# A two-layer kernel: layer 0's last FFN halves spread between layer 1's first projections, and the last batch's end in another order

## The chip, the cores and the metric

The kernel runs on one core of a Trainium2 chip. The metric is the device time of one execution in microseconds (us). A core has five engines with an instruction queue each: TensorE (PE, matrix products; its weight loads are listed apart as PEld), VectorE (DVE), ScalarE (ACT), GpSimd (POOL) and SyncE (SP), which issues most of the DMAs here. Engines run side by side and wait for each other through semaphores; each takes its own instructions strictly in order. On-chip data lie in SBUF, results of matmuls in PSUM banks of 128 x 512 fp32.

## What is computed

Four batches of 512 tokens with 512 features pass through two layers. Each layer is `x = x + s * silu(f)`, where s is a token mixer and f an FFN, both on the layer-normed x:

```python
xn = _layernorm(x)
s = _L0_attn_ref(xn, ...)          # 32 heads of 16, 8 key/value heads, softmax
g = _silu(_L0_ffn_ref(xn, ...))    # Hadamard-folded gated FFN, inner size 2048
x = x + s * g
xn = _layernorm(x)
s = _L1_attn_ref(xn, ...)          # gated delta rule, 6 heads of 64, short convolutions
g = _silu(_L1_ffn_ref(xn, ...))    # sign weights, relu, inner size 2048
x = x + s * g
```

The delta rule's recurrence over tokens, `S = S * exp(g_t) + k_t u_t`, with `u_t = b_t * (v_t - k_t S)`, is computed in four tiles of 128 tokens per batch: inside a tile by triangular inverses, between tiles through the state S.

## The kernel before

Names: NB = 4 batches, TB = 4 token tiles of 128 in a batch, NI = 16 slices of 128 of the inner size, VC = 3 slices of 128 of the 384 value columns. A Tile scheduler places the instructions: it keeps each queue's instructions close to the order in which the program lists them, and moves one past another where it takes that to be better, unless it is wrapped in `tc.keep_in_program_order`. Tiles come from pools; a tile of a pool waits until the buffer that it reuses is free, and a new pool waits until the pools whose space it takes are closed and their last readers are done.

**Layer 0.** Attention works in NU = 256 units u (64 per batch): `maxima(u)` (scores and row maxima), LAG = 11 units later `exps(u - 11)` (scores again as st, L433, and the exponentials on ACT, L435), and after every eighth `values` (L443; its sums go through DRAM and come back as the tiles oTc). The FFN is cut into as many pieces, `ffn(v, 0)` and `ffn(v, 1)` with v = u - LATE, LATE = 16: two halves in each unit, so that PE has work while DVE and ACT do the softmax. In a batch's second 32 pieces a half is one fp32 matmul of the down projection (`y<-wdn,hT`, L344; the profile lists two records for it, or four for a pair). After u = 255 there are no maxima left, and the loop goes on with the last exponentials and two halves each until `u == NU + LAG + 2`. What then is left of batch 3, four halves, four times `layer_sum` (x1 = x + s * g: four matmuls L475, a multiply on DVE L477, an add on POOL L479, a store) and four times `norm1` (statistics L61 and L62 on DVE, normalise L73, four transposes L489, a copy on ACT, a store to xn1_d, from which layer 1 loads batch 3 later), stands in `end_of_layer0()`.

**Between the layers.** `att.close()` frees the space of the attention; there the pools ce (SBUF) and cps (three PSUM banks, tiles named pu) are opened. Layer 1's first load, xn1T of batch 0 (L597), goes into ce, and so do wba and the first weights wp (L611). `projections(0)` is listed as steps with weights; then `end_of_layer0()` runs, then the steps, then `l0.close()`. Only then are c0, d0, dps and dpy opened, in which layer 1's FFN lives. There the constants upsc, drow, osc and woT are loaded on ACT's queue, and `drow * osc` (L877) is one instruction of DVE.

`projections(b)` is: `gate1(b, 2)` (L759, with the columns for the decays), `decays`, then for n = 0 to 8 `project(b, n)` (four matmuls L710, the profile shows eight records; a copy on ACT L716, three convolution steps on DVE L718, Tanh on ACT L722, a multiply on DVE L723 that ends the tile yc or yv) and `to_tokens(b, n - 1)` (four transposes L734 of yc, square and copy on ACT, a reduction on DVE), and last `gate1(b, 0)` and `gate1(b, 1)`.

**Layer 1's FFN** is a list of 128 pieces `up1(b, c)` and `down1(b, c)`, issued between the other steps: `part(count)` closes a stretch of steps in which count pieces are spread by the steps' weights. From the stretch `TAIL[1]` on, the pieces' order is pinned. `up1` begins for each batch by splitting xn1T into xsh and xsl (L892, L894). `down1(b, 15)` ends a batch: for each token tile t a multiply of y with drow (L964) into a tile named hT, of which there are two buffers, Tanh on ACT (L966), a multiply (L967) and a store to g1_d.

**The last batch's tail.** In `recurrence(3)` tile t needs `blocks32`, `blocks32b`, `blocks64` (the inverse's blocks), `with_state` (L1144, L1150: products with the state S), `new_values` (L1159, copied on ACT to Xv, L1162), `state` (S for the next tile), `outputs` (L1183), `out_norms`, `gated` (og), `project_out` (loads x1 and g1, three transposes L1222 of og, copied on ACT to ogT, L1224) and `project_out2` (six records L1233, then L1234 and L1236 on DVE and the store to out). The tiles 0 to 2 are projected out one to two steps behind the recurrence, tile 3 after it:

```python
recurrence(b)
for t in range(TB - 1, TB):
    add(0.4, project_out, NB - 1, t)
    add(2.6, project_out2, NB - 1, t)
part(len(pieces), True)
```

Of the kernel before, what the change touches and what calls it, by code (L numbers as in the profile page):

```python
# [33 lines left out]
def kernel(ctx: ExitStack, tc: tile.TileContext, i: dict, out: bass.AP):  # L34
# [66 lines left out]
    if True:  # L101
# [263 lines left out]

        sets = [(b, g) for b in range(NB) for g in range(HG)]
        NU, LAG, LATE = 8 * len(sets), 11, 16
        qds, qTs, nmxs, qms, pes = {}, {}, {}, {}, {}
# [125 lines left out]
        piece, zp = [0], []  # L494
        first_set()
# [25 lines left out]
        for u in range(NU + LATE):  # L521
            b, r = u // 64, u % 64
            v = u - LATE
            piece[0] = max(v, 0)
# [11 lines left out]
            if v >= 0:  # L536
                ffn(v, 0)
                ffn(v, 1)
# [21 lines left out]
            if u == NU + LAG + 2:  # L560
                break

        def end_of_layer0():
            for v in range(NU + LAG + 3 - LATE, NU):
                piece[0] = v
                ffn(v, 0)
                ffn(v, 1)
            for t in range(TB):
                layer_sum(NB - 1, t)
            for t in range(TB):  # L570
                norm1(NB - 1, t)
# [232 lines left out]
    def projections(b, between=(), done=None):  # L804
# [19 lines left out]
        for n in range(9):  # L824
            if done is not None and n % 2 == 0 and n < 2 * TB:
                add(0.0, gated, done, n // 2)
            prefetch()
            add(3.4, project, b, n)
            some()
            if n == 1:  # L830
                add(0.3, decay_sums, b)
            if n:
                add(0.45, to_tokens, b, n - 1)
                some()
            if done is not None and n % 2 and n < 2 * TB:
                add(0.4, project_out, done, n // 2)
                some(1)
                add(2.6, project_out2, done, n // 2)
        for m in range(VC - 1):
            prefetch()  # L840
            add(3.6, gate1, b, m)
            some()
            if m == 0:
                add(0.45, to_tokens, b, 8)
                some()
                add(0.0, norms, b)
# [4 lines left out]
    end_of_layer0()  # L851
    for _, f, args in steps:
        f(*args)
    steps.clear()
# [66 lines left out]
    pin = [False]  # L921
# [27 lines left out]

    def down1(b, c):  # L950
# [10 lines left out]
        if c == NI - 1:  # L961
            for t in range(TB):
                v = new(d0, [P, DM], F32, "hT")
                nc.vector.tensor_tensor(v, yss[b][t], drow, ALU.mult)  # L964
                th = new(d0, [P, DM], F32, "sw", bufs=3)
                nc.scalar.activation(th, v, AF.Tanh, scale=0.5)  # L966
                nc.vector.scalar_tensor_tensor(v, th, 1.0, v, ALU.add, ALU.mult)  # L967
                nc.sync.dma_start(g1_d[ds((b * TB + t) * P, P), :], v)
# [185 lines left out]
    def new_values(b, t):  # L1154
# [7 lines left out]
        nc.scalar.copy(X, px[:, :VD])  # L1162
# [30 lines left out]
    def out_norms(b, t=None):  # L1193
# [6 lines left out]
        nc.scalar.activation(so, so, AF.Sqrt)  # L1200
# [11 lines left out]

    def project_out(b, t):
        s = st[b]
        tok = ds((b * TB + t) * P, P)
        x1 = new(c0, [P, DM], F32, "x1l", bufs=2)
        nc.sync.dma_start(x1, x1_d[tok, :])
        g1 = new(c0, [P, DM], F32, "g1l", bufs=2)
        nc.sync.dma_start(g1, g1_d[tok, :])
# [5 lines left out]
        s["x1", t], s["g1", t] = x1, g1  # L1225

    def project_out2(b, t):
        s = st[b]
        tok = ds((b * TB + t) * P, P)
        x1, g1, ogT = s["x1", t], s["g1", t], s["ogT", t]  # L1230
        pf = bank()
        for m in range(VC):
            nc.tensor.matmul(pf, ogT[:, m, :], woT[:, m, :], start=(m == 0), stop=(m == VC - 1))  # L1233
        nc.vector.scalar_tensor_tensor(g1, pf, 0.5, g1, ALU.mult, ALU.mult)  # L1234
        eng = nc.vector if b >= NB - 2 else nc.gpsimd
        eng.tensor_tensor(x1, x1, g1, ALU.add)  # L1236
        nc.sync.dma_start(out[tok, :], x1)
# [18 lines left out]
    def recurrence(b, ahead=None, between=(), behind=0):  # L1256
# [9 lines left out]
        for t in range(TB + 2 if ahead is not None else TB + 1):  # L1266
# [24 lines left out]
            if 0 < t <= TB:  # L1291
                add(1.0, state, b, t - 1)
                add(1.0, outputs, b, t - 1)
                if t == TB - 1 and ahead is None:
                    add(2.0, with_state, b, t)
                    add(1.0, blocks64, b, None, t)
                if t - 1 + NZ < TB:
                    add(0.0, load_UT, b, t - 1 + NZ)
                if ahead is None:
                    if t == 3:  # L1300
                        part(TAIL[2], True)
                    add(0.0, out_norms, b, t - 1)
                    add(0.0, gated, b, t - 1)
                    for n in range(t - 3, t - 2 if t < TB else TB - 1):
                        if n >= 0:
                            add(0.4, project_out, b, n)
                            add(2.6, project_out2, b, n)
# [24 lines left out]
    for t in range(TB):  # L1332
# [6 lines left out]
        add(2.6, project_out2, b - 1, t)  # L1339
    while between:  # L1340
# [7 lines left out]
    for t in range(TB - 1, TB):  # L1348
        add(0.4, project_out, NB - 1, t)
        add(2.6, project_out2, NB - 1, t)  # L1350
# [59 lines left out]
```

## Time and profile before

| | us |
|---|---|
| median of 3 runs | 1506.74 |
| the runs | 1503.43, 1506.74, 1508.0 |
| the profiled execution | 1506.05 |
| its span | 1504.3 |
| mean granted clock of PE, as a share of full speed | 0.988 |

| stretch of the profile (us from the span's start) | PE busy, us | length, us |
|---|---|---|
| 1000 to 1100, layer 1 | 97.13 | 100 |
| 800 to 840, first projections | 28.60 | 40 |
| 840 to 880 | 38.76 | 40 |
| 1420 to 1440 | 17.18 | 20 |
| 1480 to 1504, the end | 15.95 | 24 |

How to read it: the first table compares the profiled execution with the undisturbed runs; the difference between its time and its span, 1.75 us, lies around the span. The second table gives for a stretch how long PE worked on matmuls. A stretch that PE fills can only become shorter by less work; a stretch with idle time, by letting PE wait for less. A granted clock below 1.00 makes the same matmuls longer while PE still counts as busy.

### The profile page before, as it was taken

How to read it: one execution, taken by the hardware profiler on the slowest of the kernel's cores; microseconds unless marked ns; L12 is line 12 of the kernel's file. 1: busy time of each engine (PE TensorE's matmuls, PEld its weight loads, DVE VectorE, ACT ScalarE, POOL GpSimd, SP SyncE). 2: the span in 40 equal slices, each digit the busy share in tenths (PEclk: the TensorE clock that was granted, in tenths of full speed). 3: DMA queues.
4: the chain of work that ended last, by engine and by line, in shares of the span. 5: the costliest groups of instructions: out<-in, count | busy, mean ns of one | idle time of the engine just before them, and what ended most of it. 6: DMA issues, size and time to landing. Idle time of an engine off the chain costs nothing. (4 is left out here: it accounts for less than half of the span.)

```text
span 1504.3 us, 22710 instructions
## 1 busy us (share of the span) xinstructions
PE 1434.3 (95%) x8144; PEld 856.0 (57%) x8144; DVE 1031.5 (69%) x1865; ACT 714.8 (48%) x1051; POOL 308.2 (20%) x301
## 2 busy tenths in 40 slices
PE   7999999999999999999998899999999999999997
PEld 3565533555335543456334566787568765776684
DVE  7999655765556655666516659668965799477646
ACT  4655554666446654566443424424352345323433
POOL 1122100322003210133101130054112521151000
PEclk9999999999999999999999999999999999999989
DMA  8865300474116630166014443435463354425423
GB/s 306 317 224 215 124 25 21 169 238 160 28 35 196 228 129 25 63 224 218 19 33 144 127 124 108 114 84 157 123 172 85 99 156 130 126 56 173 137 76 109
DMA packets 201793, 199.11 MB, mean 132 GB/s; under 512 B 65520, under 2 KB 153040, under 8 KB 200784
## 3 DMA queue, kind: packets, MB, share of 16 engines
q1 hardware_dynamic: 198624, 196.29, 41.4%
q10 hardware_dynamic: 3056, 1.37, 0.3%
q8 instruction: 64, 1.05, 0.3%
q14 instruction: 49, 0.40, 0.1%
HBM read 146.80 MB, written 46.19 MB: 128 GB/s over the span
## 5 line engine op out<-in xcount | busy, mean ns | idle before, releaser
L413 DVE TENSOR_REDUCE nmx<-sc 128x2 f32<-128x1024 f32 x256 | 312.1, 1219 | 160.9 <-PE st L433 149.7
L435 ACT ACTIVATE pe<-st 128x1024 f16<-128x1024 f32 x256 | 262.6, 1026 | 143.5 <-PE st L433 141.7
L344 PE MATMUL y<-wdn,hT 128*128 128x512 f32 x512 | 252.5, 617 | 3.0 <-DVE g L348 1.7
L326 PE MATMUL mm<-xr,wc 128*128 128x512 f32 x768 | 206.4, 410 | 0.0
L326 PEld LDWEIGHTS mm<-xr,wc 128*128 128x128 f32 x768 | 137.3, 189 | 48.6 <-issue 22.4
L337 POOL TENSOR_TENSOR hT<-hT,th 128x512 f32<-128x512 f32 x64 | 83.9, 1311 | 318.9 <-ACT hT L336 300.1
L344 PEld LDWEIGHTS y<-wdn,hT 128*128 128x128 f32 x512 | 87.1, 189 | 97.1 <-issue 89.7
L710 PE MATMUL pu<-xn1T,wp 128*128 128x512 f32 x288 | 133.1, 606 | 0.0
L934 PE MATMUL ph<-xsh,sg 128*128 128x512 f32 x256 | 113.6, 444 | 5.5 <-ACT sg L919 5.2
L412 PE MATMUL sc<-kT,qT 32*128 32x512 f16 x512 | 102.3, 384 | 6.3 <-DVE nmx L413 5.7
L934 PE MATMUL ph<-xsl,sg 128*128 128x512 f32 x256 | 105.5, 412 | 0.7 <-DVE xsl L894 0.7
L919 ACT ACTIVATE sg<-sw 128x512 fp32r<-128x512 f32 x128 | 79.4, 625 | 52.4 <-PE y L955 25.2
L433 PE MATMUL st<-qm,kT 32*128 32x512 f16 x512 | 100.3, 385 | 0.3 <-ACT pe L435 0.3
L459 POOL TENSOR_TENSOR oT<-os,sm 128x512 f16<-128x512 f32 x32 | 41.5, 1298 | 286.7 <-DMA sm<-rec_d 235.3
L412 PEld LDWEIGHTS <-qT 32*128 32x128 f16 x512 | 26.1, 91 | 130.0 <-issue 125.6
L710 PEld LDWEIGHTS pu<-xn1T,wp 128*128 128x128 f32 x288 | 54.9, 195 | 57.7 <-issue 55.9
L939 ACT ACTIVATE hT<-ph,upsc 128x512 f32<-128x512 f32 x64 | 43.8, 684 | 88.0 <-PE ph L934 88.0
L955 PE MATMUL y<-sg,hsh 128*128 128x512 f32 x256 | 83.9, 436 | 1.2 <-ACT sg L919 1.2
L326 PE MATMUL mm<-xr,fo 128*128 128x512 f32 x256 | 74.6, 426 | 0.5 <-DVE fo L257 0.5
L997 POOL TENSOR_TENSOR gm<-g,le 128x384 fp32r<-128x384 f32 x64 | 56.5, 901 | 88.7 <-PE pu L998 57.6
L955 PE MATMUL y<-sg,hsl 128*128 128x512 f32 x256 | 73.5, 398 | 0.0
L332 ACT ACTIVATE th<-mm,hwg 128x512 f32<-128x512 f32 x64 | 44.0, 688 | 58.3 <-PE mm L326 57.3
(291 smaller groups left out, 2364.0 us busy)
## 6 DMA issues: line engine op xcount, KB each, us to landing
wc<-wS SPq DMA_DIRECT2D x96, 512.0 KB
wS<-fo SPq DMA_DIRECT2D x16, 1024.0 KB
sw<-in_upT SPq DMA_DIRECT2D x64, 256.0 KB
sw<-in_downT SPq DMA_DIRECT2D x64, 256.0 KB
sm<-rec_d SPq DMA_DIRECT2D x128, 64.0 KB
raw<-in_w_gateT SPq DMA_DIRECT2D x8, 512.0 KB
hT<-in_w_downT SPq DMA_DIRECT2D x16, 256.0 KB
raw<-in_w_upT SPq DMA_DIRECT2D x8, 512.0 KB
```

The source lines that it names most:

```text
L326: nc.tensor.matmul(pgs[m], wcs[b, c, m][:, h, k, :], xrs[b][:, k, :], start=(k + h == 0), stop=(k == KC - 1 and h == 1))
L337: nc.gpsimd.tensor_tensor(hT, hT, ths[b, c], ALU.mult)
L344: nc.tensor.matmul(ys[t], hTs[b, c][:, ts(t, P)], wdn[:, c, :], start=(c == 0), stop=(c == NI - 1))
L412: nc.tensor.matmul(sc[:, j, :], qTs[n][rows, ts(t, P)], kTs[b, g // 4][rows, :], start=True, stop=True)
L413: nc.vector.tensor_reduce(nmxs[n][:, t, 2 * pr : 2 * pr + 2], sc, AX.X, ALU.max, negate=True)
L433: nc.tensor.matmul(st[:, j, :], kTs[b, g // 4][rows, ts(k, P)], qms[n][rows, :], start=True, stop=True)
L435: nc.scalar.activation(pes[u], st, AF.Exp)
L710: nc.tensor.matmul(pp, wps[b, n][:, k, 0:P], xn1Ts[b][:, k, :], start=(k == 0), stop=(k == KC - 1))
L919: tc.keep_in_program_order(nc.scalar.activation(sgs[b, c, m], raws[b, c, m], AF.Sign))
L934: ins = nc.tensor.matmul(ph, sgs[b, c, 0][:, ts(k, P)], xss[b][n][:, k, :], start=(k + n == 0), stop=(k == KC - 1 and n == 1))
L955: ins = nc.tensor.matmul(yss[b][t], hss[b, c][n][:, ts(t, P)], sgs[b, c, 1], start=(c + n == 0), stop=(c == NI - 1 and n == 1))
L997: nc.gpsimd.tensor_tensor(gm, bc_in(s["g2"][:, t, u, x], P), bc_mid(le, 3), ALU.mult)
```

## The change

**Layer 0's end.** `halves(u)` gives the number of halves issued before unit u. Up to u = NU it is two per unit as before; from there one per unit, and the loop ends at NU + LAG. The list `rest` holds the twenty halves left over, then the four `layer_sum` and the four `norm1`; they are called between the steps of `projections(0)`, in proportion to 1.5 times the steps' weights, so that `rest` is used up after two thirds of them. `end_of_layer0` is gone; `l0.close()` still comes after the steps.

**The last batch's end.** `project_out` is split: `out_loads` takes the loads of x1 and g1, `out_sum` the last multiply, the add and the store. For the last batch:

- `down1(3, 15)` only multiplies y with drow, pinned, into four buffers (two of hT, two of hsh). The rest of the piece, `gate_y2` (Tanh, multiply, store of g1), and `out_loads` come for all four tiles in a later step. The loads for tiles 2 and 3 go into the freed tile of xn1T.
- `project_out` of tiles 0 and 1 comes ahead of the last `with_state`; `project_out2` of tiles 0 to 2 comes after the last `outputs`, and `out_sum` behind it, pinned; its result banks are those of y (dpy) instead of pu.
- Tile 3's X is copied on DVE instead of ACT; Sqrt in `out_norms` of tiles 2 and 3 is pinned.
- The adds of `out_sum` run on POOL for tiles 0 to 2 and on DVE for tile 3.
- The weight of `blocks64` in the last stretch is 4 instead of 1, the stretch `TAIL[2]` ends at t = 3 behind the last `blocks64`, and `out_norms` and `gated` of tile 2 are listed after it.

```diff
+        def halves(u):
+            return 2 * (min(max(u, LATE), NU) - LATE) + max(u - NU, 0)
...
+        def half(h):
+            piece[0] = h // 2
+            ffn(h // 2, h % 2)
...
-        for u in range(NU + LATE):
+        for u in range(NU + LAG + 1):
...
-            if v >= 0:
-                ffn(v, 0)
-                ffn(v, 1)
+            for h in range(halves(u), halves(u + 1)):
+                half(h)
...
-            if u == NU + LAG + 2:
-                break
-        def end_of_layer0():
...
+        rest = [(half, h) for h in range(halves(NU + LAG + 1), 2 * NU)]
+        rest += [(f, NB - 1, t) for f in (layer_sum, norm1) for t in range(TB)]
...
     projections(0)
-    end_of_layer0()
-    for _, f, args in steps:
+    total, done, n = sum(x[0] for x in steps), 0.0, 0
+    for w, f, args in steps:
         f(*args)
+        done += w
+        while n < len(rest) and n < 1.5 * len(rest) * done / total:
+            rest[n][0](*rest[n][1:])
+            n += 1
     steps.clear()
     l0.close()
...
+    def gate_y2(b, t, v):
+        th = new(d0, [P, DM], F32, "sw", bufs=3)
+        piece_order(nc.scalar.activation(th, v, AF.Tanh, scale=0.5))
+        nc.vector.scalar_tensor_tensor(v, th, 1.0, v, ALU.add, ALU.mult)
+        nc.sync.dma_start(g1_d[ds((b * TB + t) * P, P), :], v)
...
+                if b == NB - 1 and t > 1:
+                    vs.append(new(d0, [P, DM], F32R, "hsh").bitcast(F32))
+                else:
+                    vs.append(new(d0, [P, DM], F32, "hT"))
+                if b < NB - 1:
+                    gate_y(b, t, vs[t])
+                else:
+                    piece_order(nc.vector.tensor_tensor(vs[t], yss[b][t], drow, ALU.mult))
...
-        nc.scalar.copy(X, px[:, :VD])
+        if (b, t) == (NB - 1, TB - 1):
+            nc.vector.tensor_copy(X, px[:, :VD])
+        else:
+            nc.scalar.copy(X, px[:, :VD])
...
+        pf = s["pf", t] = bank() if b < NB - 1 else new(dpy, [P, DM], F32, f"y{t}")
...
+    def out_sum(b, t):
+        s = st[b]
+        x1, g1 = s["x1", t], s["g1", t]
+        ins = nc.vector.scalar_tensor_tensor(g1, s["pf", t], 0.5, g1, ALU.mult, ALU.mult)
+        if b == NB - 1:
+            tc.keep_in_program_order(ins)
+        eng = nc.vector if b == NB - 2 or (b, t) == (NB - 1, TB - 1) else nc.gpsimd
+        eng.tensor_tensor(x1, x1, g1, ALU.add)
+        nc.sync.dma_start(out[ds((b * TB + t) * P, P), :], x1)
...
+            if t == TB and ahead is None:
+                for n in range(TB):
+                    add(0.0, lambda n=n: gate_y2(b, n, yvs[b][n]))
+                    add(0.0, out_loads, b, n)
+                for f, n in ((out_norms, 2), (gated, 2), (outputs, 3), (project_out2, 0), (project_out2, 1),
+                             (project_out, 2), (out_norms, 3), (gated, 3), (out_sum, 0), (out_sum, 1),
+                             (project_out2, 2), (out_sum, 2)):
+                    add(1.0, f, b, n)
+            elif 0 < t <= TB:
...
                 if t == TB - 1 and ahead is None:
+                    add(0.0, project_out, b, 0)
+                    add(0.0, project_out, b, 1)
                     add(2.0, with_state, b, t)
-                    add(1.0, blocks64, b, None, t)
+                    add(4.0, blocks64, b, None, t)
...
-    for t in range(TB - 1, TB):
-        add(0.4, project_out, NB - 1, t)
-        add(2.6, project_out2, NB - 1, t)
+    for f in (project_out, project_out2, out_sum):
+        add(1.0, f, NB - 1, TB - 1)
     part(len(pieces), True)
```

More of the change, by code (lines that the diff above doesn't have):

```diff
@@ L519 @@
             early.setdefault(q, []).append(lambda q=q: mix_down(q))
-        for u in range(NU + LATE):
+        for u in range(NU + LAG + 1):
             b, r = u // 64, u % 64
             v = u - LATE
-            piece[0] = max(v, 0)
+            piece[0] = halves(u) // 2
             if v == 32:
@@ L559 @@
                     keys_values(b + 1)
-            if u == NU + LAG + 2:
-                break
-        def end_of_layer0():
[L564 to L571, printed above, removed]
+        rest = [(half, h) for h in range(halves(NU + LAG + 1), 2 * NU)]
+        rest += [(f, NB - 1, t) for f in (layer_sum, norm1) for t in range(TB)]
     att.close()
@@ L838, in projections @@
                 add(2.6, project_out2, done, n // 2)
+                add(0.0, out_sum, done, n // 2)
         for m in range(VC - 1):
@@ L919, in signs @@
             tc.keep_in_program_order(nc.scalar.activation(sgs[b, c, m], raws[b, c, m], AF.Sign))
-    pin = [False]
+    pin, yvs = [False], {}
     def piece_order(ins):
@@ L948, in up1, with gate_y @@
             hss[b, c] = split(hT, [P, SEQ], "hs")
+    def gate_y(b, t, v):
+        nc.vector.tensor_tensor(v, yss[b][t], drow, ALU.mult)
+        gate_y2(b, t, v)
+    def gate_y2(b, t, v):
[3 more added lines that the diff above has]
+        nc.sync.dma_start(g1_d[ds((b * TB + t) * P, P), :], v)
     def down1(b, c):
@@ L961, in down1 @@
         if c == NI - 1:
+            vs = []
             for t in range(TB):
[L963 to L968, printed above, removed]
+                if b == NB - 1 and t > 1:
[6 more added lines that the diff above has]
+                    piece_order(nc.vector.tensor_tensor(vs[t], yss[b][t], drow, ALU.mult))
+            yvs[b] = vs
     for m in range(2):
@@ L1199, in out_norms @@
         nc.vector.tensor_scalar(so, so, 1.0 / HD, EPS, ALU.mult, ALU.add)
-        nc.scalar.activation(so, so, AF.Sqrt)
+        ins = nc.scalar.activation(so, so, AF.Sqrt)
+        if b == NB - 1 and t >= TB - 2:
+            tc.keep_in_program_order(ins)
         nc.vector.reciprocal(so, so)
@@ L1211, in gated, with out_loads @@
         eng.tensor_tensor(og, o, og, ALU.mult)
+    def out_loads(b, t):
+        s = st[b]
+        tok = ds((b * TB + t) * P, P)
+        if b == NB - 1 and t >= 2:
+            if t == 2:
+                s["xg"] = new(ce, [P, KC, SEQ], F32, "xn1T")
+            x1, g1 = (s["xg"][:, 2 * t - 4 + n, :] for n in range(2))
+        else:
+            x1 = new(c0, [P, DM], F32, "x1l", bufs=2)
+            g1 = new(c0, [P, DM], F32, "g1l", bufs=2)
+        nc.sync.dma_start(x1, x1_d[tok, :])
+        nc.sync.dma_start(g1, g1_d[tok, :])
+        s["x1", t], s["g1", t] = x1, g1
     def project_out(b, t):
         s = st[b]
[L1215 to L1219, printed above, removed]
+        if b < NB - 1:
+            out_loads(b, t)
         pz = bank()
@@ L1224, in project_out @@
         nc.scalar.copy(ogT, v3(pz))
-        s["x1", t], s["g1", t] = x1, g1
     def project_out2(b, t):
         s = st[b]
-        tok = ds((b * TB + t) * P, P)
-        x1, g1, ogT = s["x1", t], s["g1", t], s["ogT", t]
-        pf = bank()
+        pf = s["pf", t] = bank() if b < NB - 1 else new(dpy, [P, DM], F32, f"y{t}")
         for m in range(VC):
-            nc.tensor.matmul(pf, ogT[:, m, :], woT[:, m, :], start=(m == 0), stop=(m == VC - 1))
-        nc.vector.scalar_tensor_tensor(g1, pf, 0.5, g1, ALU.mult, ALU.mult)
-        eng = nc.vector if b >= NB - 2 else nc.gpsimd
+            nc.tensor.matmul(pf, s["ogT", t][:, m, :], woT[:, m, :], start=(m == 0), stop=(m == VC - 1))
+    def out_sum(b, t):
+        s = st[b]
+        x1, g1 = s["x1", t], s["g1", t]
+        ins = nc.vector.scalar_tensor_tensor(g1, s["pf", t], 0.5, g1, ALU.mult, ALU.mult)
+        if b == NB - 1:
+            tc.keep_in_program_order(ins)
+        eng = nc.vector if b == NB - 2 or (b, t) == (NB - 1, TB - 1) else nc.gpsimd
         eng.tensor_tensor(x1, x1, g1, ALU.add)
-        nc.sync.dma_start(out[tok, :], x1)
+        nc.sync.dma_start(out[ds((b * TB + t) * P, P), :], x1)
     def solve(b):
@@ L1290, in recurrence @@
             next_other()
-            if 0 < t <= TB:
+            if t == TB and ahead is None:
[7 more added lines that the diff above has]
+            elif 0 < t <= TB:
                 add(1.0, state, b, t - 1)
@@ L1294, in recurrence @@
                 if t == TB - 1 and ahead is None:
+                    add(0.0, project_out, b, 0)
+                    add(0.0, project_out, b, 1)
                     add(2.0, with_state, b, t)
-                    add(1.0, blocks64, b, None, t)
+                    add(4.0, blocks64, b, None, t)
                 if t - 1 + NZ < TB:
                     add(0.0, load_UT, b, t - 1 + NZ)
-                if ahead is None:
-                    if t == 3:
-                        part(TAIL[2], True)
+                if ahead is None and t == TB - 1:
+                    part(TAIL[2], True)
+                elif ahead is None:
                     add(0.0, out_norms, b, t - 1)
                     add(0.0, gated, b, t - 1)
[L1304 to L1307, printed above, removed]
             some(4)
@@ L1339 @@
         add(2.6, project_out2, b - 1, t)
+        add(0.0, out_sum, b - 1, t)
     while between:
```

## The prediction

> **What bounds the kernel now.** I read the busy shares first, then the forty slices, then the stretches around the two edited places as a table of windows, and inside those the timeline of TensorE (PE) and the chain of waits.
>
> ```profile
> PE 1434.3 (95%) x8144; PEld 856.0 (57%) x8144; DVE 1031.5 (69%) x1865; ACT 714.8 (48%) x1051; POOL 308.2 (20%) x301
> ...
> PE   7999999999999999999998899999999999999997
> ```
>
> PE is the bound nearly everywhere, so a change can win only where PE idles or runs at a lower clock. Outside the first slice two places show it: around 800 us (layer 0's end and layer 1's first projections) and the last 100 us. The diff edits both.
>
> ```profile
> 759.09:786.80 27.71, 27.66 (x102) 9.28 (x100) 1.96 (x4) 12.63 (x14) 1.27 (x1) 1.00 0.07 16
> 786.80:796.53 9.73, 9.73 (x27) 4.36 (x26) 0.40 (x2) 1.39 (x3) 1.21 (x6) 1.00 0.72 195
> 796.53:870.36 73.83, 62.31 (x264) 37.80 (x263) 54.33 (x121) 30.82 (x52) 12.49 (x17) 0.93 0.41 127
> ...
> 1449.25:1504.30 55.05, 45.32 (x385) 32.75 (x384) 35.38 (x80) 19.46 (x33) 1.82 (x2) 0.97 0.28 90
> ```
>
> Columns: stretch, length, busy time of PE, PEld, DVE, ACT, POOL, then the granted clock. The first row is layer 0's last exponentials, the second the halves held back for the load of layer 1's input, the third goes from the first gate1 to the end of gate1(1), the fourth is the tail. The third loses 73.83 - 62.31 = 11.52 us to idle PE, the fourth 55.05 - 45.32 = 9.73. PE's rows say to whom:
>
> ```profile
> 814.20 0.66 PE L734 MATMUL pu<-identf,yc 128*128 128x128 f32 x4 [3.51 <-DVE yc L723]
> 814.69 5.29 PE L710 MATMUL pu<-xn1T,wp 128*128 128x512 f32 x8
> 821.88 1.11 PE L489 MATMUL mm<-identf,xn 128*128 128x128 f32 x8 [1.89 <-DVE xn L73]
> ...
> 825.28 3.60 PE L710 MATMUL pu<-xn1T,wp 128*128 128x512 f32 x8
> ...
> 837.81 1.12 PE L734 MATMUL pu<-identf,yc 128*128 128x128 f32 x4 [5.06 <-DVE yc L723]
> 838.72 5.51 PE L710 MATMUL pu<-xn1T,wp 128*128 128x512 f32 x8
> ```
>
> The bracket is PE's idle time and its releaser. Eight L710 matmuls take 3.60 us at full clock and 5.29 and 5.51 behind the long waits: 1.7 + 1.9, about 3.6 us, lost to the clock. The 3.51 came about because DVE did layer_sum and the statistics of norm1 (L477, L61, 0.66 each) ahead of yc; the 5.06 because DVE stood at drow for a load:
>
> ```profile
> 836.67 0.48 DVE L877 TENSOR_SCALAR drow<-drow,osc 128x512 f32<-128x512 f32 x1 [4.25 <-DMA osc<-in_output_scale]
> ```
>
> In the tail:
>
> ```profile
> 1485.66 1.55 PE L1183 MATMUL pu<-Xv,W 128*128 128x64 f32 x12 [2.24 <-ACT Xv L1162]
> 1487.05 0.50 PE L1222 MATMUL pu<-identf,og 128*128 128x128 f32 x3
> 1488.12 4.30 PE L1233 MATMUL pu<-woT,ogT 128*128 128x512 f32 x6 [0.57 <-ACT ogT L1224]
> 1492.25 0.49 PE L1222 MATMUL pu<-identf,og 128*128 128x128 f32 x3
> 1493.37 2.84 PE L1233 MATMUL pu<-woT,ogT 128*128 128x512 f32 x6 [0.62 <-ACT ogT L1224]
> ```
>
> By the chain of waits the 2.24 is a detour: a g1 store held one of the two hT buffers for 2.78 us (1479.23), the third drow multiply waited for it, two Tanh with a table load followed on ACT, and the Xv copy was queued behind them.
>
> **Change, part A: the end of layer 0.** In the order of the changed program PE has 16 halves among the last exponentials instead of 22. A pair of halves is a 1.98 us row, so six fewer end the values about 5.85 us earlier. Eleven exponentials at 1.03 us on ACT (mean of L435) with their matmuls (0.39) and hand-overs need about 1.6 each, 17.6 in all, below the 21.9 that remain, so ACT does not become the bound. Were the chain 2.2 each, 24.2 in all, 2.3 us of the saving would go.
>
> Then PE waits for layer 1's input. Its load was issued at 786.90, right as the values ended, and gate1's weights, queued on SP behind the wait for wba, were there at 795.3: 8.5 us, covered by ten halves and the first layer_sum. Now six halves and six L475 matmuls, 6.65 us, cover it: 1.9 us of new idle time. gate1 starts 5.85 + 9.73 (the second row) - 8.55 = 7.0 us earlier.
>
> From there to the end of gate1(1): PE's work at full clock was 62.31 - 3.6 = 58.7. Ten halves come in, 9.7 (at 0.96 to 0.99 each); 25 of FFN1's matmuls (nine and eight of L934, eight of L955, 0.23 apart, 5.75 us) go out, because d0, dps and dpy open only when l0 closes, after the last norm1. That gives 62.6. The waits that I place along the new order: the 3.51 goes, because halves stand there and yc is ahead of layer_sum on DVE; norm1's transposes wait about 2.4 (DVE has four statistics and the 1.22 cast before the normalise), and three yc waits of 0.6, 0.85 and 0.9 stay: 4.75. The drow stall moves with l0's closing to about 65 us after gate1's start, where DVE is less urgent and three PSUM banks are full: between 0 and 4.25, I take 1.5, as a wait there reaches PE only through the banks. One drop of the clock costs 0 or 1.7; I take 1.7, for this reason:
>
> ```profile
> 1418.84 0.50 PE L934 MATMUL ph<-xsh,sg 128*128 128x512 f32 x1 [2.15 <-ACT sg L919]
> ...
> 1420.00:1422.00 2.00, 2.00 (x6) 1.13 (x4) 0.00 (x0) 0.00 (x0) 0.00 (x0) 0.50 0.32 51
> ```
>
> A wait of 2.15 us was followed by a granted clock of 0.50. The 1.89 before L489 was not (the clock stayed at 1.00). The 2.4 is nearer to the first.
>
> The Trainium skill (TensorE: Matmul & The Clock Gate, HAM oscillation) puts the limit at idle gaps over about 3.4 us; by that page none of my new waits would lower the clock and the sum would be 1.7 us better. The row above, with less idle time and a lower clock, does not fit that limit.
>
> So 62.6 + 4.75 + 1.5 + 1.7 = 70.5 instead of 73.8: 3.3 less. The FFN1 work that left comes back in a stage where PE is 95 to 98% busy, at 5.75 / 0.977 = 5.9. A = -7.0 - 3.3 + 5.9 = -4.4. Bounds: no waits, stall or drop, -12.3; all old waits (11.5) and drops (3.6) again with the whole 4.25 stall, +7.
>
> **Part B: the tail.** PE's work does not change. Up to the last L1233's end it idles 5.39 us now (0.77, 0.57, 2.24, 0.57, 0.62, 0.62) and loses 1.46 to the clock (4.30 against 2.84). The new order removes the cause of the 2.24: the drow multiplies go into four buffers, all before the Tanhs, and X is copied on DVE. The first two transposes of og are done earlier, so PE finds other work during most copies of ogT. What I still count is 0.2 + 0.25 + 0.45 + 0.1 + 0.35 and, for the last two, 0.55 twice: 2.45. B = 2.45 - 5.39 - 1.46 = -4.4. Bounds: only the last two remain, -5.8; the same sum in other places, 0.
>
> What hides the rest: the four g1 stores go out on SP in a row and each load follows its store; one store took 2.78 us, so the loads land about 5 us before the last L1233 ends. With that cover gone, each us of lateness is one at the end, as nothing but the sums stands behind them on DVE. Three adds go to POOL (1.35 each, median of eight, against 0.69 on DVE), done about 0.9 us before the last sum.
>
> A DVE multiply with both inputs in SBUF took 1.18 us instead of 0.558 while POOL multiplied (L1147 at 1453.51, POOL L1173 at 1453.29). I take nothing for it here, at most 0.6 after the 0.9 is used up.
>
> The Trainium skill (SBUF — State Buffer, Who interferes with whom) speaks against those adds: a DVE instruction with two SBUF inputs contends with a GpSimd instruction that reads SBUF. If the last add had to wait for a whole POOL add, the end would be about 0.4 us later.
>
> **Sum.** 1506.05 (the profiled run; its span 1504.3 and 1.75 around it) - 8.8 = 1497.3. That run lies 0.7 under the median of 1506.74, so 1498.0 for the median.
>
> **Rivals.**
> - *The projections close up further.* DVE was busy 54.33 of 73.83 us, so there is room. With only the 2.4 left, A = -7.0 - (73.8 - 65.0) + 5.9 = -9.9 and the time about 1492.5. Against it: each yc has a chain through ACT and DVE that halves cover only in five places.
> - *New waits replace the old ones.* The edit moves layer_sum and norm1 among later projections but takes no work from DVE. If they cost PE the same 11.5 + 3.6, A = -7.0 + (62.6 + 15.1 - 73.8) + 5.9 = +2.8; with the tail's -4.4 the time is about 1505, not distinguishable from no change.
> - *Slower: DVE sets the pace of projections 4 to 8.* Its statistics, casts (1.22 and 2.29) and normalises now stand between the yc of five projections. The mean of the old pair is 4.3 us idle and 1.8 of clock, 6.1. Four of these, plus the 1.5, make 25.9 instead of 7.95: +18 - 8.8, about 1516. It decides from some 16.8 us of waits and lost clock. Against it: DVE's whole block is about 8 us, and it was paid in two lumps before.
> - *The tail does not do what it says*: the g1 loads, queued on SP behind four stores, land over 4 us late, and B is 0: about 1502.4.
>
> **How the numbers follow.** Forecast 0.52, closing up 0.13, new waits 0.14, tail without gain 0.08, slower 0.13. About 0.3%, 4.5 us, is what a measurement can tell from no change. The forecast, the closing up and a little of the tail case are faster by more than that: 0.66; the rest of the tail case and the new waits lie within it: 0.21; slower 0.13. The forecast's own range is 1494 to 1502. With the first two rivals the range is 1490 to 1507; that leaves out the slower case and a little on the other side.
>
> **What would show it.** In the new profile: the values end about 781, PE idles about 2 us before gate1 near 789.5; no wait of 3.5 us before the first yc transposes; one of some 2.4 before norm1's; DVE waits for osc later, PE hardly; no wait for Xv in the tail, and 4.3 us from the last L1233's end to the span's end as now. Wrong would be: clock under 0.9 over the 70 us after gate1, FFN1 returning at less than 5.9, or a DVE wait for a g1 load at the last sums.

## The result and the profile after

The changed kernel takes 1491.82 us in the median of six runs (1489.07 to 1496.63), the kernel before 1505.51 in six runs beside it (1502.08 to 1508.0): a ratio of 0.9914, 95% interval 0.9897 to 0.9932. A second comparison gave 1496.56 against 1508.32, 0.9927 (0.9904 to 0.9949). The change makes the kernel faster by 12 to 14 us. The forecast was 1498.0, a gain of 8.8, in a range of 1490 to 1507: the direction held, and the gain was larger than forecast. The narrower range that the prediction gave to its own sum, 1494 to 1502, holds the second comparison and not the first.

The profiled execution took 1494.06 us, 12.0 less than that of before; its span is 1492.3. From the table of windows, the stretches that answer to the four of before (layer 0's last exponentials end at 783.1; then the cover of the load, the projections up to the end of gate1(1), and the tail):

```profile
783.09:791.59 8.50, 6.66 (x21) 2.81 (x19) 1.09 (x3) 1.07 (x3) 1.22 (x6) 1.00 0.70 194
791.59:860.90 69.31, 63.99 (x258) 38.58 (x259) 52.36 (x116) 26.52 (x47) 13.46 (x17) 0.95 0.42 125
1438.00:1492.30 54.30, 47.91 (x404) 35.26 (x402) 35.20 (x82) 19.36 (x35) 5.68 (x5) 0.99 0.28 92
```

The columns are those of before: stretch, length, busy time of PE, PEld, DVE, ACT, POOL, granted clock. The projections now lose 5.32 us to idle PE instead of 11.52, the tail 6.4 instead of 9.7; the cover of the load, which had no idle time, has 1.84.

PE's timeline of the changed kernel where the projections stalled before (start, duration, line, operation, and in brackets idle time and releaser):

```profile
784.43 5.31 PE L344 MATMUL y<-wdn,hT 128*128 128x512 f32 x12
791.59 4.05 PE L760 MATMUL pu<-wp,xn1T 128*128 128x140 f32 x32 [1.84 <-DMA wp<-in_wg1T]
795.48 7.03 PE L711 MATMUL pu<-xn1T,wp 128*128 128x512 f32 x16
803.02 0.37 PE L697 MATMUL pu<-g,le 128*128 128x24 f32 x2 [0.51 <-DVE g L683]
...
803.68 1.96 PE L344 MATMUL y<-wdn,hT 128*128 128x512 f32 x4
805.48 0.60 PE L735 MATMUL pu<-identf,yc 128*128 128x128 f32 x4
805.92 3.60 PE L711 MATMUL pu<-xn1T,wp 128*128 128x512 f32 x8
...
835.06 0.63 PE L735 MATMUL pu<-identf,yc 128*128 128x128 f32 x4 [1.03 <-DVE yc L724]
835.52 3.60 PE L711 MATMUL pu<-xn1T,wp 128*128 128x512 f32 x8
840.67 1.11 PE L495 MATMUL mm<-identf,xn 128*128 128x128 f32 x8 [1.54 <-DVE xn L73]
```

In four places halves (L344) stand between a projection (L711, L710 before) and the transposes (L735) of the tile yc that DVE finishes meanwhile. There is no wait of 3.5 or 5 us any more, and eight L711 records take 3.60, where two of these groups took 5.29 and 5.51; one group, at 844.72, takes 4.15 beside a stretch of half clock. And the drow multiply, for which DVE stood 4.25 us:

```profile
855.65 0.49 DVE L884 TENSOR_SCALAR drow<-drow,osc 128x512 f32<-128x512 f32 x1 [0.29 <-DMA osc<-in_output_scale]
```

The end of the tail, PE:

```profile
1472.43 1.45 PE L1181 MATMUL pu<-R,U 128*128 128x64 f32 x12
1473.72 2.79 PE L1269 MATMUL y<-woT,ogT 128*128 128x512 f32 x6
1476.35 1.45 PE L1208 MATMUL pu<-Xv,W 128*128 128x64 f32 x12
1477.63 2.79 PE L1269 MATMUL y<-woT,ogT 128*128 128x512 f32 x6
1480.31 0.52 PE L1260 MATMUL pu<-identf,og 128*128 128x128 f32 x3
1481.40 2.84 PE L1269 MATMUL y<-woT,ogT 128*128 128x512 f32 x6 [0.57 <-ACT ogT L1262]
1484.08 0.49 PE L1260 MATMUL pu<-identf,og 128*128 128x128 f32 x3
1485.14 2.84 PE L1269 MATMUL y<-woT,ogT 128*128 128x512 f32 x6 [0.57 <-ACT ogT L1262]
```

The copy of X (between L1181 and L1208) is hidden behind an output projection; only the last two ogT copies are waited for.

To see where the 12 us lie, the same events of each profile are set against each other: us from one of layer 0's last score matmuls, ahead of everything that the edit touches (744.58 in before, 745.50 after). V is the end of layer 0's last values, G the first gate1, P the end of gate1(1), N1 the first new_values of batch 1, N2 that of batch 2's last tile, N3 that of batch 3's tile 1, E the end of the last output projection. Each number is a difference of two starts or ends in the trace.

| kernel | V | G | P | N1 | N2 | N3 | E | E - N3 |
|---|---|---|---|---|---|---|---|---|
| before | 42.25 | 51.95 | 125.77 | 398.83 | 610.15 | 712.97 | 755.42 | 42.45 |
| after | 37.66 | 46.09 | 115.39 | 392.43 | 603.69 | 705.32 | 742.48 | 37.16 |
| after, once more | 37.66 | 46.14 | 112.54 | 395.46 | 606.81 | 707.05 | 744.19 | 37.14 |
| layer 0's end alone | 37.67 | 45.83 | 112.07 | 390.79 | 602.84 | 706.87 | 749.46 | 42.59 |
| tail alone | 42.25 | 51.95 | 127.62 | 400.99 | 612.99 | 717.38 | 754.49 | 37.11 |
| all before the projections | 37.67 | 52.67 | 125.50 | 397.08 | 609.00 | 712.21 | 749.35 | 37.14 |
| two halves, rest spread | 42.25 | 50.76 | 120.52 | 396.47 | 608.64 | 711.87 | 748.97 | 37.10 |
| wba early | 38.17 | 44.76 | 110.82 | 388.91 | 600.07 | 704.95 | 742.08 | 37.13 |
| wba early, once more | 38.16 | 44.89 | 111.41 | 393.53 | 604.76 | 705.19 | 742.33 | 37.14 |
| sums before the last halves | 38.37 | 45.08 | 118.40 | 396.43 | 608.47 | 708.74 | 745.85 | 37.11 |

Of the first profile's 12.0 us, 6.4 are there at N1 and 5.3 come in the tail; between N1 and N2 nothing changes (211.3 in both), 1.2 come between N2 and N3, where the clock is at half speed for 13.65 us instead of 17.07, and 0.9 are lost ahead of the edit. The column E - N3 repeats within 0.15 us. The columns from P to N3 scatter by 3 us between the two profiles of the changed kernel: up to P the clock is the reason, behind it a wait for DVE as well (see the section on the prediction and the last one).

### The profile page after: what moved, and what is told of

The parts are those of the page before. It is cut to its first block, busy times and chain, and to the rows that moved or that the text cites. A ratio compares the mean times of both kernels' runs of the same rounds, so it can differ in the third digit from the quotient of the medians.

```text
span 1492.3 us, 22700 instructions
## 1 busy us (share of the span) xinstructions
PE 1429.4 (96%) x8144; PEld 855.6 (57%) x8144; DVE 1035.8 (69%) x1863; ACT 709.6 (48%) x1046; POOL 313.5 (21%) x304
## 5 line engine op out<-in xcount | busy, mean ns | idle before, releaser
L344 PE MATMUL y<-wdn,hT 128*128 128x512 f32 x512 | 253.3, 617 | 3.0 <-DVE g L348 1.7
L344 PEld LDWEIGHTS y<-wdn,hT 128*128 128x128 f32 x512 | 87.0, 189 | 96.0 <-issue 88.5
L711 PE MATMUL pu<-xn1T,wp 128*128 128x512 f32 x288 | 129.9, 594 | 0.0
L711 PEld LDWEIGHTS pu<-xn1T,wp 128*128 128x128 f32 x288 | 54.0, 191 | 56.6 <-issue 54.8
L1019 POOL TENSOR_TENSOR gm<-g,le 128x384 fp32r<-128x384 f32 x64 | 57.8, 921 | 83.0 <-PE pu L1020 52.0
```

Of the source, the lines that this page charges most:

```text
L344: nc.tensor.matmul(ys[t], hTs[b, c][:, ts(t, P)], wdn[:, c, :], start=(c == 0), stop=(c == NI - 1))
L711: nc.tensor.matmul(pp, wps[b, n][:, k, 0:P], xn1Ts[b][:, k, :], start=(k == 0), stop=(k == KC - 1))
L1019: nc.gpsimd.tensor_tensor(gm, bc_in(s["g2"][:, t, u, x], P), bc_mid(le, 3), ALU.mult)
```

## The experiments

**Layer 0's end alone, and the tail alone.** The two halves of the diff, each put on the kernel before; no line of either is changed.

> Only the edit of layer 0's end, with the tail of before. Theory: the two edits are independent and the first is worth 5 to 6.5 us of the 13, so 1499 to 1501 against 1505.5 (ratio 0.9957 to 0.9967); in the profile gate1(1) ends about 9.5 us earlier than in before and 4 of these come back with FFN1's deferred pieces. Rival: the first edit is worth nothing by itself, since the deferred FFN1 pieces come back in full and its gain was one of the clock; then the ratio is 0.999 to 1.001.

> Only the edit of the last batch's end, with layer 0's end of before. Theory: 5 to 6.5 us, ratio 0.9957 to 0.9967, with no wait for Xv over 0.5 us in the tail; with the kernel that has the first edit alone it makes up the whole. Rival: the tail gains only where FFN1 was deferred by the first edit, because the deferred pieces fill its waits; then the ratio is 0.998 or more.

Layer 0's end alone: 1497.66 us (six runs) against 1506.19, ratio 0.9949 (0.9931 to 0.9967). The tail alone: 1497.88 (nine runs), ratio 0.9955 (0.9939 to 0.9970). The product is 0.9904, inside the interval of the whole: as far as these intervals can tell, the two gains add up. In the table the first has 8.0 us at N1 and none of the tail's gain, the second all of the tail's gain and nothing at V and G. Both rivals fall.

**Which part of layer 0's end does it.** First the spreading is taken away, then the thinning of the last exponentials; the tail stays changed.

```diff
+    for x in rest:
+        x[0](*x[1:])
     for w, f, args in steps:
         f(*args)
-        done += w
-        while n < len(rest) and n < 1.5 * len(rest) * done / total:
...
```

> The changed kernel, but all of the list rest runs ahead of the steps of projections(0): one half per unit among the last exponentials, nothing spread. Theory: the spreading does the work, so the gain of layer 0's end is gone and the wait for yc comes back: about 5 us over the changed kernel, ratio to before 0.9945 to 0.997. Rival: it is the earlier end of the exponentials that counts (the load starts earlier and is still covered); then the ratio stays at 0.991 to 0.9925.

1497.34 us, ratio 0.9943 (0.9927 to 0.9958): as fast as with the tail alone. PE fills the load's time with all sixteen halves, and then waits as before:

```profile
782.89 13.89 PE L344 MATMUL y<-wdn,hT 128*128 128x512 f32 x32
...
813.15 1.39 PE L495 MATMUL mm<-identf,xn 128*128 128x128 f32 x8 [2.96 <-DVE xn L73]
...
821.98 0.62 PE L697 MATMUL pu<-g,le 128*128 128x24 f32 x2 [5.19 <-DVE g L683]
```

gate1 starts no earlier than in before, though the values end 4.6 us earlier. The long wait is the one for the decay sums this time: their small DVE steps (L670 to L683) are queued between those of norm1, of yc and of the split into xsh and xsl.

```diff
-            return 2 * (min(max(u, LATE), NU) - LATE) + max(u - NU, 0)
+            return 2 * (max(u, LATE) - LATE)
```

> The changed kernel, but with two halves per unit to the end of the loop as in before; only the eight halves that are then left, layer_sum and norm1 are spread. Theory: the load of layer 1's input is uncovered (1 to 3 halves instead of 6 and six layer_sum matmuls in its 8.5 us), PE idles some 6 us before gate1, and the waits of the later projections are filled by fewer halves: 4 to 7 us over the changed kernel, ratio 0.994 to 0.996. Rival: what counts is that layer_sum and norm1 leave DVE's way in the first projections; then it stays within 1.5 us of the changed kernel, 0.991 to 0.9925.

1495.28 us, ratio 0.9933 (0.9918 to 0.9949), an interval that overlaps those of the changed kernel; in its one profile it lies 4.0 us over the changed kernel at N1. The loss is at the lower end of what was expected or under it, and its place was not as expected: the scheduler put eight halves ahead of gate1, where the expectation had one to three, and PE waits only 1.44 us for the weights. The price came later:

```profile
782.50 7.13 PE L344 MATMUL y<-wdn,hT 128*128 128x512 f32 x16
791.08 4.05 PE L760 MATMUL pu<-wp,xn1T 128*128 128x140 f32 x32 [1.44 <-DMA wp<-in_wg1T]
...
827.16 0.63 PE L735 MATMUL pu<-identf,yc 128*128 128x128 f32 x4 [2.21 <-DVE lnmv L62]
...
849.22 1.11 PE L735 MATMUL pu<-identf,yv 128*128 128x128 f32 x4 [5.63 <-DVE yv L724]
```

With only one pair of halves left for the projections, layer_sum and norm1 come early and run into the middle ones. At N1 the thinning alone is worth 1.8 us (398.83 to 397.08) and the spreading alone 2.4 (to 396.47), where both gave 6.4; but these are single profiles, and N1 scatters by more than that. PE's idle time between G and P is a steadier measure: 11.52 and 11.58 us in the two profiles with the old end of layer 0, 4.96 to 5.35 in seven profiles with the new one, 9.70 with everything ahead of the projections and 10.71 with two halves per unit. With either part undone most of the waits are back: thinning is what leaves halves to spread, and spreading is what puts them where PE waits.

**What the tail's 5.3 us are.** Four kernels, one profile each, read by E - N3 (37.16 in the changed kernel, 42.45 before). They ran on one chip whose single run of before took 1511.82, so their times are not compared with the others'.

```diff
-        if (b, t) == (NB - 1, TB - 1):
-            nc.vector.tensor_copy(X, px[:, :VD])
-        else:
-            nc.scalar.copy(X, px[:, :VD])
+        nc.scalar.copy(X, px[:, :VD])
```

> The changed kernel, but tile 3's X is copied on ACT as in before. The stretch from the first new_values matmul of tile 1 to the end of the last output projection was 42.45 us before and 37.16 after. Theory: the wait of 2.24 us went because the Tanhs and the drow multiplies no longer stand ahead of the copy, not because of the engine: 37.1 to 37.6. Rival: the engine is what matters; the copy waits for ACT as before and the stretch is 39 to 40.

38.37, between the two. The wait for X did not come back, so its engine is not what removed the 2.24. But PE waits 1.10 us for og of tile 2 (the trace says "issue"; DVE ends og at 1485.90 and the transposes start 0.10 us later, as they do in the changed kernel): ACT, after the copy, loads the Tanh table, does the four Tanhs and loads the table again, all ahead of the pinned Sqrt of tile 2's norm.

```diff
-        eng = nc.vector if b == NB - 2 or (b, t) == (NB - 1, TB - 1) else nc.gpsimd
+        eng = nc.vector if b >= NB - 2 else nc.gpsimd
```

> The changed kernel, but all last adds run on DVE. From the end of the last output projection to the last add 1.39 us pass if nothing is in DVE's way. Theory: no difference of more than 0.3 us, since the three adds are done before the last projection ends on either engine. Rival (POOL's adds and DVE's sums get in each other's way): the DVE operations of the last 8 us become shorter and the end 0.4 to 1.2 us earlier.

37.13, and from the end of the last projection to the end of the last add 1.46 us, where the changed kernel has 1.45: no difference. In the changed kernel POOL's three adds run from 1483.74 to 1487.45 and DVE's last sum starts at 1488.02, 0.69 long as ever.

```diff
-                if b == NB - 1 and t > 1:
-                    vs.append(new(d0, [P, DM], F32R, "hsh").bitcast(F32))
-                else:
-                    vs.append(new(d0, [P, DM], F32, "hT"))
...
+                vs.append(new(d0, [P, DM], F32, "hT"))
+                gate_y(b, t, vs[t])
...
-                    add(0.0, lambda n=n: gate_y2(b, n, yvs[b][n]))
```

> The changed kernel, but the end of the last down1 as in before: two hT buffers, Tanh, multiply and store of g1 at once for each tile. Theory: the third drow multiply waits for the first store again, 2 to 3 us, DVE stands in front of the copy of X, and PE waits 1.5 to 3 us for it: the stretch that was 37.16 becomes 39 to 41, and with a drop of the clock up to 42.5. Rival: it was the order of the projections that mattered; 37.2 to 37.8.

41.78: the two buffers bring back 4.6 of the 5.3 us. The price was forecast, the path was not. DVE did copy X first; the third drow multiply came at 1485.12, behind the first two stores (SP issued them from 1482.03), and its Tanh stands ahead of the Sqrt on ACT. ACT's and PE's timelines of this kernel:

```profile
1485.83 1.36 ACT L963 ACTIVATE sw<-hT 128x512 f32<-128x512 f32 x2 [1.62 <-DVE hT L958]
1487.21 1.28 ACT L1219 ACT_TABLE_LOAD   x1
1488.50 0.21 ACT L1219 ACTIVATE so<-so 128x6 f32<-128x6 f32 x1
```

```profile
1490.42 0.52 PE L1254 MATMUL pu<-identf,og 128*128 128x128 f32 x3 [3.06 <-issue]
1491.51 4.28 PE L1263 MATMUL y<-woT,ogT 128*128 128x512 f32 x6 [0.57 <-ACT ogT L1256]
```

PE waits 3.06 us for the transposes of og, and the next projection runs at half clock (4.28 instead of 2.84): 3.06 + 1.44 = 4.5. The trace puts the wait down to "issue"; that it is og follows from what the transposes read, from ACT's rows, and from DVE's og, which ends 0.10 us before them.

```diff
-                    add(0.0, project_out, b, 0)
-                    add(0.0, project_out, b, 1)
                     add(2.0, with_state, b, t)
...
-                for f, n in ((out_norms, 2), (gated, 2), (outputs, 3), (project_out2, 0), (project_out2, 1),
-                             (project_out, 2), ...
+                for f, n in ((out_norms, 2), (gated, 2), (outputs, 3), (project_out, 0), (project_out2, 0),
+                             (project_out, 1), (project_out2, 1), (project_out, 2), ...
```

> The changed kernel, but project_out of tiles 0 and 1 comes after the last outputs instead of ahead of the last with_state. Theory: PE has nothing between the last new_values and outputs and waits for the copy of X, 0.5 to 0.9, and for one ogT more, 0.6: the stretch that was 37.16 becomes 38.2 to 38.8. Rival: the transposes are covered wherever they stand; under 37.6.

41.07, 3.9 over the changed kernel where 1.0 to 1.6 were expected. The waits are the expected ones, and the clock is added to them:

```profile
1475.62 2.00 PE L1208 MATMUL pu<-Xv,W 128*128 128x64 f32 x12 [1.07 <-DVE Xv L1185]
1477.40 1.49 PE L1260 MATMUL pu<-identf,og 128*128 128x128 f32 x6
1478.82 5.97 PE L1269 MATMUL y<-woT,ogT 128*128 128x512 f32 x12
1485.46 0.55 PE L1260 MATMUL pu<-identf,og 128*128 128x128 f32 x3 [0.67 <-DVE og L1238]
```

Behind a wait of 1.07 us the outputs take 2.00 instead of 1.45, the transposes 1.49 instead of 0.82. So the reordering of the projections and the four buffers each take away a wait long enough to lower the clock, and with either one undone most of the gain is gone.

**Can the 1.84 us before gate1 be had?** SP's queue in the changed kernel: the load of gate1's weights stood 4.0 us waiting for the landing of wba, a load of 48 columns on ACT's queue. In this kernel wba is loaded during layer 0 into a tile of the pool cst.

```diff
+        wba = new(cst, [P, KC, 2 * NH], F32, "wba")
+        nc.scalar.dma_start(wba[:, :, 0:NH], i["wb1T"].rearrange("(k p) n -> p k n", p=P))
+        nc.scalar.dma_start(wba[:, :, NH:], i["wa1T"].rearrange("(k p) n -> p k n", p=P))
...
-    wba = new(ce, [P, KC, 2 * NH], F32, "wba")
...
```

> The changed kernel, but wba is loaded during layer 0 into a buffer of its own, so that the load of gate1's weights has nothing ahead of it on SP that waits for wba. In the changed kernel PE idles 1.84 us before gate1. Theory: the wait for wba's landing (4.0 us in SP's queue) is what made the weights late; without it they land some 3 to 4 us earlier, before PE's cover ends, the 1.84 go, and the kernel is about 1.8 us faster than the changed one (ratio to before 0.989 to 0.9915, within the noise of one comparison; the profile decides). Rival: the load of xn1T, issued as the values end, takes as long; the wait before gate1 stays above 1 us.

In the second kernel layer_sum comes earlier as well:

```diff
-        rest += [(f, NB - 1, t) for f in (layer_sum, norm1) for t in range(TB)]
+        rest[-4:-4] = [(layer_sum, NB - 1, t) for t in range(TB - 1)]
+        rest += [(layer_sum, NB - 1, TB - 1)] + [(norm1, NB - 1, t) for t in range(TB)]
```

> As the kernel with the early wba, but layer_sum of tiles 0 to 2 is listed ahead of the last four halves, so that DVE and POOL have less to do between the last layer_sum and norm1. Theory: norm1's waits of PE (1.54 + 0.46) shrink to under 1 us and the whole is 1 to 1.5 us faster than with the early wba alone. Rival: the halves are missing at the earlier projections, whose yc waits come back; no gain or up to 2 us lost.

The wait before gate1 is gone in the first (SP issues the weights' load 1.3 us after that of xn1T instead of 5.3), and G comes 1.3 us earlier. Its ratio is 0.9925 (0.9898 to 0.9951). The second came out at 0.9947 (0.9929 to 0.9965), which is not clear of the first by time alone; in its profile norm1's waits shrink to 1.1 us, but a yv wait of 5.5 us appears, with the clock at half speed for 10.2 us, and PE idles 9.20 us between G and P instead of 4.98. Its rival is the better account. The first was then run once more beside the changed kernel:

> The changed kernel once more, beside the kernel with the early wba on one chip. Its ratio to before should lie in 0.9897 to 0.9932 again, as in the first comparison; in the profile PE waits 1.6 to 1.9 us for gate1's weights.

> The kernel with the early wba once more. Theory: 1.9 us faster than the changed kernel on the same chip, if the 1.84 us of waiting is all that differs; the single runs of both spread over 7 us, so medians of the same chip should differ by 0 to 4. Rival: no difference, because the clock's drops swallow it; then the medians are within 1 us or the other way round.

On that chip the changed kernel took 1496.56 us, with PE waiting 1.89 us before gate1 again, and the one with the early wba 1498.32 us, ratios 0.9927 (0.9904 to 0.9949) and 0.9935 (0.9917 to 0.9954). The rival of the last expectation held, and no gain can be told: 1.3 us are less than what the clock and the wait for DVE behind P vary by from run to run. The early wba takes away a wait; that it makes the kernel faster isn't shown.

## Why the prediction was right, and where its sizes were off

**The rival "the projections close up further" came nearest in time (1492.5 against 1491.8), but not by its own working.** It had A = -9.9 and the tail as forecast. Seven profiles have this edit unaltered: three in the table of events and those of the four tail experiments. Measured at N1, A was -3.4 to -8.0 in them, -5.9 in the mean (forecast -4.4); the tail brought -5.3. That A came out near its forecast is in part luck: the values saved less than forecast, the projections much more, and more came back behind them.

**Values' end.** Forecast 5.85 us earlier, measured 4.6 (42.25 to 37.66, the same within 0.01 in all seven). The sixteen halves are there. But six of them stand alone, 1.06 us from start to start instead of 0.96, and the 32 matmuls of the last values come in nine groups instead of four, 3.7 us instead of 2.7.

**The load.** Forecast 8.5 us and 1.9 of idle time; measured 8.50 and 1.84. gate1 starts 5.9 us earlier instead of 7.0, and all of the difference is that of the values.

For what follows, the two profiles with the old end of layer 0 and the seven with the new one, in us. "vb" is the time of four DVE multiplies (L1012) that follow drow; "PE behind P" is PE's wait for DVE in head_products of batch 0, right behind gate1(1).

| kernel | G to P | PE idle in it | half clock in it | DVE's wait for osc | vb | PE behind P | P to N1 | half clock in it |
|---|---|---|---|---|---|---|---|---|
| before | 73.83 | 11.52 | 10.24 | 4.25 | 1.94 | 0 | 273.06 | 0 |
| tail alone | 75.67 | 11.58 | 13.65 | 3.87 | 1.94 | 0 | 273.37 | 0 |
| after | 69.30 | 5.32 | 6.83 | 0.29 | 1.95 | 0 | 277.04 | 0 |
| after, once more | 66.39 | 5.31 | 0 | 2.74 | 3.86 | 2.76 | 282.93 | 6.83 |
| layer 0's end alone | 66.24 | 5.16 | 0 | 1.76 | 2.59 | 0.56 | 278.72 | 0 |
| X on ACT | 67.81 | 5.06 | 3.41 | 1.41 | 2.58 | 0.55 | 280.34 | 3.41 |
| adds on DVE | 66.37 | 5.29 | 0 | 2.47 | 3.22 | 1.66 | 279.97 | 0 |
| two buffers | 66.43 | 5.35 | 0 | 2.56 | 3.22 | 1.65 | 279.44 | 0 |
| late transposes | 66.04 | 4.96 | 0 | 3.03 | 3.85 | 2.76 | 281.15 | 3.41 |

**The projections, the most mis-sized term.** Forecast 3.3 us shorter (70.5 us), measured 4.5 to 7.8 (66.04 to 69.30). Three parts of the sum were too large.

- The work: without idle time, and with half of the half-clock time taken off, 60.6 to 61.1 us where I had 62.6. The ten halves are 1.0 of this: 8.7 us from start to start where I charged 9.7. Another 0.5 lies in the reading of before: the two stretches at half clock, 815.25 to 818.66 and 835.73 to 842.56, hold 3.41 and 4.75 us of busy PE, and half of that, 4.1, was lost, where two groups of L710 alone gave 3.6.
- The waits: I placed 4.75 and added 1.5 for the drow stall, 6.25. The profile has 0.51, 1.03, 1.54 + 0.46, 1.24 and 0.53, 5.3 in all, with norm1's 2.0 where 2.4 was forecast. The drow stall did not reach PE within this stretch.
- The clock: one drop at 1.7 was charged. Five of the seven profiles have none here, one has one and one has two.

**The drow stall** came behind P instead. DVE's wait for osc was 0.29 to 3.03 us, within the bounds of 0 to 4.25 and 2.0 in the mean where I took 1.5. Where it is long, PE waits long in head_products. The matmuls there read yc and write a pu bank, and what released them is cth (L765), which reads such a bank; so the wait went through the banks, as forecast, but in the next stage. It is more than the stall itself, as DVE's rows show, first of the changed kernel, then of its second profile:

```profile
856.66 1.95 DVE L1012 TENSOR_TENSOR vb<-z,hb 128x384 f32<-128x384 f32 x4
```

```profile
855.53 0.49 DVE L884 TENSOR_SCALAR drow<-drow,osc 128x512 f32<-128x512 f32 x1 [2.74 <-DMA osc<-in_output_scale]
...
856.53 3.86 DVE L1012 TENSOR_TENSOR vb<-z,hb 128x384 f32<-128x384 f32 x4
```

Where vb takes 1.95, POOL only fills tiles beside it (until 857.48; its next multiply starts at 861.15). Where it takes 2.6 to 3.9, POOL's multiplies gm (L1019) run beside it, in the second profile from 856.94 to 858.87 and again from 859.13. The sum had no term for this.

**FFN1 coming back** cost less than forecast. I charged 5.75 / 0.977 = 5.9 for the 25 matmuls that leave the projections, arguing from a stage that is 95 to 98% busy. P to N1 grew by 4.0 to 9.9. Without PE's wait behind P and half of the half-clock time, 3.6 to 5.3 are left, 4.5 in the mean and under 5.9 in all seven. The tables of windows for the stretch from P to the first gate1 of batch 1, and from there to its last ones, show why; before, and then after:

```profile
870.36:891.08 20.72, 18.72 (x132) 12.34 (x131) 12.54 (x25) 6.55 (x13) 11.86 (x14) 1.00 0.34 92
891.08:955.18 64.10, 62.48 (x243) 39.90 (x242) 58.72 (x158) 31.01 (x55) 3.25 (x4) 1.00 0.42 119
```

```profile
860.90:886.65 25.75, 24.13 (x153) 16.76 (x153) 17.96 (x32) 8.22 (x16) 12.87 (x14) 1.00 0.48 131
886.65:949.98 63.33, 63.12 (x247) 40.73 (x246) 58.34 (x157) 31.42 (x56) 2.75 (x4) 1.00 0.38 112
```

Before, PE idled 2.00 + 1.62 = 3.62 us there, after 1.62 + 0.21 = 1.83. The deferred pieces were placed into waits, and 5.75 - 1.8 = 4.0. From P to N1 as a whole, PE idled 7.02 and 7.21 us with the old end of layer 0; with the new one it idled 4.8 to 5.7, the wait behind P left out. A stage that is 97% busy still has gaps, and work with no due time can go into them.

**The tail.** Forecast -4.4, measured -5.3. The waits left up to the last projection are 0.34 for the Xv of tile 2 and twice 0.57, 1.5 in all where I counted 2.45; the others of 0.1 to 0.45 don't occur, and that is the difference. Which edit does it was told incompletely: the prediction gave the 2.24 to the buffers and the copy's engine together, and the experiments give it to the buffers (4.6 with their clock drop) and to the early transposes (3.9 with theirs), which overlap in the end; the engine is worth 1.2, through ACT's queue and not through X.

**The rivals.** "New waits replace the old ones" is what the kernel with everything before the projections does, and the one with the sums ahead of the last halves; not this one. "DVE sets the pace" falls for the projections: DVE was busy for 52.36 of 69.31 us and PE's longest wait for it is 1.54 (behind P it is up to 2.76). "The tail does not do what it says" falls: SP has issued the last g1 loads by 1480.2, and DVE's sums of tiles 0 and 1 run at 1482.98 without a wait for a DMA.

**The two rules weighed.** The 0.4 us that the prediction derived from the Trainium skill (SBUF — State Buffer, Who interferes with whom) were rightly left out of the sum: with the adds on DVE nothing changes, since POOL is done before DVE's last pair. The rule itself, that a DVE instruction with two SBUF inputs contends with a GpSimd instruction that reads SBUF, agrees with the rows of vb above, 1.95 us without POOL's multiplies and up to 3.86 with them. The same skill's limit of about 3.4 us of idle time (TensorE: Matmul & The Clock Gate, HAM oscillation) does not fit these profiles: the drop in the kernel with the late transposes came behind a wait of 1.07.

## What to carry to other kernels

Work that can run at any time is worth most where another engine's chain is the limit: first see which waits end last, then keep that work back for them, and lay it between the steps rather than ahead of them. Work that is pushed out of one stage can cost less than its length, by as much as it fills of the waits in the stage that takes it (here 4.5 us of 5.75), so read those waits before charging it in full. A stall that is moved can surface a stage later, so follow it there. And when a queue-ordered engine such as ACT serves several chains, a buffer that is one too few can show as a wait on quite another chain.

## What the runs showed of the hardware

The granted clock changes at fixed periods, and not by the length of one gap. In all fourteen profiles every stretch at half clock that the span's end does not cut is 3.41 us long or a multiple (6.83, 10.24, 13.65), and within a profile all of them begin a whole number of 3.41 us apart. Laid back to back from the first drop, these periods can be read one by one. Four of the changed kernel, two around the wait before gate1 and the two ahead of the drops in the projections:

| period (us from the span's start) | PE idle in it, us | granted clock in the next |
|---|---|---|
| 787.80 to 791.22 | 1.47 | 1.00 |
| 791.22 to 794.63 | 0.37 | 1.00 |
| 839.00 to 842.42 | 2.00 | 0.50 |
| 852.66 to 856.07 | 1.77 | 0.50 |

In the third period two waits for norm1 add up (1.54 + 0.46), in the fourth 1.24 and 0.53. The wait of 1.84 us before gate1 was longer than any of these waits, but a border cut it into 1.47 and 0.37, and the clock stayed at 1.00. Counted over all fourteen profiles (worked out from the traces): the clock fell after 64 periods, none with less than 0.96 us of idle PE; it stayed up after some 5880, none with more than 2.01; and it rose again only after periods with at most 0.48. Between 0.96 and 2.01 it went either way: 43 periods were followed by a drop and 136 were not. So the idle time of a period, as these traces give it, does not decide alone, and what else does is not shown.

A drop costs about 1.7 us, half of a period. At P the seven profiles with the new end of layer 0 show it: five without a drop since V lie at 112.07 to 112.62, the one with one at 114.00, the one with two at 115.39. Behind P the wait for DVE adds its 0 to 2.8 us.
